# Experts on TensorE: seven f32 products of quarter blocks against three single-pass products of 12-bit parts

## The chip, the cores and the metric

The kernel runs on one core of one Trainium2 chip. The metric is the device time of one execution in microseconds (us), from runs of the unchanged program; lower is better. A separate profiled execution gives the trace. The engines are TensorE (PE; its weight load is listed apart as PEld), VectorE (DVE), ScalarE (ACT), GpSimd (POOL) and SyncE (SP), which issues the transfers.

## What is computed

Two layers work on x of shape (8, 256, 32, 32), all in f32.

```python
# layer 0: softmax attention with a depthwise convolution, then a gated FFN with an 8x8 block FFT filter
x = conv_layer(x, ...)
# layer 1, on tokens t = (8, 1024, 256)
t = t + causal_attention(ln(t), WQ, WK, WV)
z = ln(t)                                     # layer norm over the 256 channels
w = softmax(mean(z, axis=0) @ Wr + br)        # per token position, 8 experts
h = relu(bn1(einsum('bfd,edh->bfeh', z, W1) + b1))
h = relu(bn2(einsum('bfeh,ehk->bfek', h, W2) + b2))
y = einsum('bfeh,ehd->bfed', h, Wo) + bo
t = t + einsum('bfed,fe->bfd', y, w)
```

All 8 experts are computed for all 8192 tokens; each has three 256x256 matrices. The experts' output scaling by w can be done on the second layer's output, because the third layer is linear.

## The kernel before

A tile holds 128 partitions; 256 channels are two groups k of 128 (KC = 2). Work is issued through wrappers (`InOrder`, lines 59 to 73) that keep each of PE, DVE, ACT and POOL in the order in which the code asks for it; most records therefore carry line 71. Transfers are asked for with `nc.sync.dma_start`, all on SyncE's queue, and are not held in this way: a planner places them where their buffers and data are ready.

Layer 0 (lines 476 to 1214) makes the first x. It uses the type F32R for a few products: the scores take queries and keys cut into a high and a low part (`queries_keys`, `stack`, `attend`).

Layer 1's attention (lines 1251 to 1521) goes over 8 images b. `causal(b)` makes scores, exponentials, their normalisation, transposes and the product with the values, row block by row block. Beside it `beside(b)` runs `first_norm(b + 1)`, `second_norm(b - 1)` and `keys_values(b + 1)`. `together(main, side, 0.85)` mixes the two by planned costs that the steps yield: the side gets 0.85 us of its steps per us of the main ones, and what is left of it follows when the main ones are done. `second_norm` makes z = ln(t), stores it to `z_d` and t to `u_d` in device memory, and adds z to `feat` for the gate. The last image is done in halves (`second_norm_half`), then `gate` makes the weights w in `wT`. `load_experts()` loads all 24 expert matrices at the start of this stage.

The experts (lines 1536 to 1769) go over 128 pieces: halves (h, b) of 512 tokens, h outermost, and in each the 8 experts. A piece has `layer1`, `layer2` two pieces later and `layer3` four pieces later; in each pass of the loop at line 1741 four steps of these three are interleaved, and vector work put off in `soon` follows each step. `by_seven` forms a 256x256 by 256x512 product from seven products of 128x128 by 128x256 instead of eight, with sums of the weight blocks (`weight_sums`) and of the column blocks (`column_sums`). Layers 1 and 3 do so for every expert, layer 2 for the odd ones; for even experts layer 2 is four f32 products of 512 columns. Layer 3 adds all 8 experts up in four PSUM banks; `close` then combines them, adds them to t and stores the output. `fetch` loads z and t of a half, three buffers each.

Of the kernel before, what the change touches and what calls it, by code (L numbers as in the profile page):

```python
# [9 lines left out]
F32 = mybir.dt.float32  # L10
F32R = mybir.dt.float32r
BF16 = mybir.dt.bfloat16
# [13 lines left out]
NE = 8  # L26
# [10 lines left out]
MOE_EPS = 1e-3  # L37

# [65 lines left out]
def conv_attn_hybrid_kernel(  # L104
# [1121 lines left out]
    z_d = [dram.tile([P, KC, N], F32, tag=f"zd{b}", name=f"zd{b}") for b in range(B)]  # L1226
# [10 lines left out]
    w_of = []  # L1237
    for e in range(NE):
        w_of.append([])
        for name in ("w1", "w2", "wo"):  # L1240
            w_ = wm.tile([P, KC, C], F32, tag=f"{name}_{e}", name=f"{name}_{e}")
            w_of[e].append(w_)

    def load_experts():
        for e in range(NE):
            for w_, src in zip(w_of[e], (w1, w2, wo)):
                nc.sync.dma_start(w_, src[e].rearrange("(k p) o -> p k o", p=P))
# [3 lines left out]
    with ExitStack() as l1:  # L1251
# [34 lines left out]
        load_experts()  # L1286
# [78 lines left out]
        def second_norm(b):  # L1365
            yield from until((b, N // QC - 1))
            z2 = two.tile([P, KC, N], F32, tag="z2", name="z2", bufs=1)
            yield from layer_norm(b, z2)
            nc.sync.dma_start(z_d[b], z2)
            nc.sync.dma_start(u_d[b], t[b])  # L1370
            if b + 3 < B:
                load_t(b + 3)
            if b == 0:
                pool.tensor_copy(feat, z2)
            else:
                pool.tensor_add(feat, feat, z2)

        def second_norm_half(b, h):
# [6 lines left out]
            nc.sync.dma_start(z_d[b][:, :, hs], z2)  # L1385
            nc.sync.dma_start(u_d[b][:, :, hs], t[b][:, :, hs])
            yield 0.5

# [105 lines left out]
        def beside(b):  # L1494
            if b + 1 < B:
                yield from first_norm(b + 1)
            if b >= 1:
                yield from second_norm(b - 1)
            if b + 1 < B:
                yield from keys_values(b + 1)  # L1500
            else:
                yield from second_norm_half(b, 0)
                yield from gate(0)

# [14 lines left out]
        for steps in (second_norm_half(B - 1, 1), gate(1)):  # L1519
            for _ in steps:  # L1520
                pass
# [14 lines left out]
    with ExitStack() as l2:  # L1536
# [4 lines left out]
        s1, o1 = bn_fold("g1", "be1", "m1", "v1", eps_moe, "bn1", extra="b1")  # L1541
        s2, o2 = bn_fold("g2", "be2", "m2", "v2", eps_moe, "bn2", extra="b2")
# [20 lines left out]
        sums_of = [[None] * 3 for _ in range(NE)]  # L1563

        def seven(e):

            return e % 2 == 1

        def weight_sums(eng, e):

            for l in (0, 1, 2) if seven(e) else (0, 2):
                w_ = w_of[e][l]
                s_ = sums_of[e][l] = hp.tile([P, 3, P], F32, tag=f"ws{e}_{l}", name=f"ws{e}_{l}", bufs=1)
                a11, a21, a12, a22 = (w_[:, k, g * P : (g + 1) * P] for k in range(KC) for g in range(KC))
                eng.tensor_add(s_[:, 0, :], a21, a22)
                eng.tensor_sub(s_[:, 1, :], s_[:, 0, :], a11)
                eng.tensor_sub(a21, a11, a21)
                eng.tensor_sub(s_[:, 2, :], a12, s_[:, 1, :])

        def column_sums(src, name):  # L1580

            T = hp.tile([P, 4, QC], F32, tag=name, name=name, bufs=3 if name == "t2" else 2)
            B4 = src.rearrange("p k (c n) -> p (k c) n", n=QC)
            dve.tensor_sub(T[:, 0:2, :], B4[:, 1::2, :], B4[:, 0:2, :])
            dve.tensor_add(T[:, 2, :], T[:, 1, :], B4[:, 0, :])
            dve.tensor_sub(T[:, 3, :], B4[:, 2, :], T[:, 2, :])
            return T

        def pairs(e, l, src, T):

            w_, s_ = w_of[e][l], sums_of[e][l]
            a11, s3, a12, a22 = (w_[:, k, g * P : (g + 1) * P] for k in range(KC) for g in range(KC))
            b11, b21, b22 = src[:, 0, :QC], src[:, 1, :QC], src[:, 1, QC:]
            return [
                [(s_[:, 0, :], T[:, 0, :]), (a11, b11)],
                [(a12, b21), (s_[:, 1, :], T[:, 2, :])],
                [(s_[:, 2, :], b22), (s3, T[:, 1, :])],
                [(a22, T[:, 3, :])],
            ]

        halves = [(h, b) for h in range(2) for b in range(B)]
        pieces = [(h, b, e) for h, b in halves for e in range(NE)]
        zs, ts, tz, gate_of, bias_of, h1_of, h2_of, acc_of = {}, {}, {}, {}, {}, {}, {}, {}
# [4 lines left out]
        def fetch(i):  # L1608
            if i < len(halves):
                h, b = halves[i]  # L1610
                for of, src, name in ((zs, z_d, "z"), (ts, u_d, "t")):
                    of[h, b] = hp.tile([P, KC, HALF], F32, tag=name, name=f"{name}e", bufs=3)
                    nc.sync.dma_start(of[h, b], src[b][:, :, cut(h)])

        def gate_rows(h, e):

            wb = gate_of[h, e] = hp.tile([P, HALF], F32, tag=f"wb{e}", name=f"wb{e}", bufs=1)
            pw = ps_b.tile([P, HALF], F32, tag="pm", name="pw")
            pe.matmul(pw, sel8[:, e, :], wT[:, cut(h)], start=True, stop=True)
            act.copy(wb, pw)  # L1620

        def gated_bias(h):

            gb = bias_of[h] = hp.tile([P, KC, HALF], F32, tag="gb", name="gb", bufs=1)
            for g in range(KC):
                pw = ps_b.tile([P, HALF], F32, tag="pm", name="pg")
                pe.matmul(pw, boT[:, g, :], wT[:, cut(h)], start=True, stop=True)
                act.copy(gb[:, g, :], pw)

        soon = [[], [], []]  # L1630

        def by_seven(plan, dst, scale, bias, space, tag):

            first = hp.tile([P, 2, QC], F32, tag="first", name="first", bufs=3)

            def of(i):
                pm = space.tile([P, 2, QC], F32, tag=tag, name=f"{tag}{i}")
                for j, (lhs, rhs) in enumerate(plan[i]):
                    pe.matmul(pm[:, j, :], lhs, rhs, start=True, stop=True)
                return pm  # L1640

            def both(x):
                return x.unsqueeze(1).to_broadcast([P, 2, QC])

            act.copy(first, of(0))
            yield
            dve.tensor_add(dst[:, 0:2, :], of(1), both(first[:, 1, :]))
            yield
            dve.tensor_add(dst[:, 2:4, :], of(2), both(dst[:, 1, :]))
            dve.tensor_add(dst[:, 1, :], dst[:, 2, :], first[:, 0, :])  # L1650
            act.activation(dst[:, 0:2, :], dst[:, 0:2, :], AF.Relu, bias=bias[:, 0:1], scale=scale[:, 0:1])
            yield
            dve.tensor_add(dst[:, 2, :], dst[:, 3, :], of(3)[:, 0, :])
            dve.tensor_add(dst[:, 3, :], dst[:, 3, :], first[:, 0, :])
            act.activation(dst[:, 2:4, :], dst[:, 2:4, :], AF.Relu, bias=bias[:, 1:2], scale=scale[:, 1:2])

        def layer1(h, b, e):

            h1 = hp.tile([P, 4, QC], F32, tag="h1", name="h1", bufs=3)
            c = slice(KC * e, KC * e + 2)  # L1660
            yield from by_seven(pairs(e, 0, zs[h, b], tz[h, b]), h1, s1[:, c], o1[:, c], ps_a, "pa")
            h1 = h1.rearrange("p (k c) n -> p k (c n)", k=KC)
            h1_of[h, b, e] = h1, None

            def sums():
                h1_of[h, b, e] = h1, column_sums(h1, "t1")

            if seven(e):
                soon[2].append(sums)
            yield  # L1670

        def layer2(h, b, e):
            h1, T = h1_of.pop((h, b, e))
            h2 = hp.tile([P, KC, HALF], F32, tag="h2", name="h2", bufs=3)
            if seven(e):
                c = slice(KC * e, KC * e + 2)
                h2_4 = h2.rearrange("p k (c n) -> p (k c) n", n=QC)
                yield from by_seven(pairs(e, 1, h1, T), h2_4, s2[:, c], o2[:, c], ps_b, "pm")
            else:
                w_ = w_of[e][1]  # L1680
                for g in range(KC):
                    pm = ps_b.tile([P, HALF], F32, tag="pm", name="pm")
                    for k in range(KC):
                        pe.matmul(pm, w_[:, k, g * P : (g + 1) * P], h1[:, k, :], start=(k == 0), stop=(k == KC - 1))
                    c = KC * e + g
                    act.activation(h2[:, g, :], pm, AF.Relu, bias=o2[:, c : c + 1], scale=s2[:, c : c + 1])
                    if g == 0:
# [194 lines left out]
```

## Time and profile before

| | us |
|---|---|
| median of 3 runs | 3311.7 (3303.55 to 3316.38) |
| profiled execution | 3302.11 |
| its span, first to last instruction | 3300.4 |
| busy in the span: PE / PEld / DVE / ACT / POOL | 3043.3 / 2066.2 / 2346.7 / 1395.4 / 361.1 |
| mean granted TensorE clock | 0.966 |

The busy time of PE counts records whose ends are modelled; it tells where PE has work, not that it is at its peak. In the page's slices each digit is the busy share in tenths of one fortieth of the span (82.5 us): layer 0 fills the first 17, layer 1's attention starts at about 1430 us, and the experts' first product is at 2076.4 us. In a list of groups a line reads: code line, engine, operation, output<-inputs, shapes, count | busy us, mean ns of one | idle us before them and what ended it.

### The profile page before, as it was taken

To read this page: it belongs to the slowest core of one execution; us is meant where nothing else is said; L and a number is where in the kernel's file an instruction comes from. 1 tells how busy PE (TensorE), PEld (TensorE's weight loads), DVE (VectorE), ACT (ScalarE), POOL (GpSimd) and SP (SyncE) were. 2 spreads that over 40 slices of the span, in tenths; PEclk is the share of its full clock that TensorE was granted. 3 is DMA by queue.
4 is the path that set the end of the run, shared out by engine and by line. 5 is a ranking of instruction groups with operands and counts; after the bars stand their busy time and mean duration, and the time that the engine had idled before them with its cause. 6 is when DMAs were issued, how large, how long until landed. Compare 5 with 4: busy or idle time off the path is not lost.

```text
span 3300.4 us, 43194 instructions
## 1 busy us (share of the span) xinstructions
PE 3043.3 (92%) x17462; PEld 2066.2 (63%) x17462; DVE 2346.7 (71%) x3710; ACT 1395.4 (42%) x2168; POOL 361.1 (11%) x482
## 2 busy tenths in 40 slices
PE   5998999999998998769999998999999999999999
PEld 3554555454555455346565665678777777778787
DVE  1377877787877786835544444688888877888887
ACT  2554454545454544323333332344444444444443
POOL 1121212020212010001122212400000000000000
PEclk8998999999999999879999999899999999999999
DMA  4202030303030300030111101100000000000000
GB/s 146 71 8 77 26 77 27 77 27 77 27 77 27 77 14 7 16 136 26 47 44 39 39 26 52 42 24 20 20 20 20 32 16 23 20 20 26 13 7 13
DMA packets 44596, 130.60 MB, mean 40 GB/s; under 512 B 3862, under 2 KB 12134, under 8 KB 40550
## 3 DMA queue, kind: packets, MB, share of 16 engines
q1 hardware_dynamic: 44390, 127.78, 12.5%
q8 instruction: 139, 2.28, 0.3%
q14 instruction: 67, 0.55, 0.1%
HBM read 77.17 MB, written 50.59 MB: 39 GB/s over the span
## 4 chain that ended last, share of the span: by engine, by line
PE 49%; DVE 5%; ACT 1%; POOL 1%; issue 1%; DMA 0%; SPq 0%; ACTq 0%; POOLq 0%; DVEq 0%
PE pm L71 12%; PE pa L71 12%; PE q L71 11%; PE s L71 4%; PE po L71 3%; PE pk L71 2%; PE pv L71 2%; DVE nm L71 1%; DVE zt L71 1%; DVE pr L71 1%; DVE st L71 1%; ACT pr L71 1%; PE tp L71 1%; PE tpz L71 1%; PE tpt L71 1%
## 5 line engine op out<-in xcount | busy, mean ns | idle before, releaser
L71 ACT ACTIVATE h<-h,bn_o,bn_s 128x512 f32<-128x512 f32 x384 | 308.6, 813 | 631.2 <-DVE h L71 631.1
L71 DVE SCALAR_TENSOR_TENSOR x<-hpad,vec,x 128x1024 f32<-128x1024 f32 x248 | 317.1, 1283 | 39.9 <-ACT x L71 32.9
L71 DVE SCALAR_TENSOR_TENSOR conv<-hpad,vec,conv 128x1024 f32<-128x1024 f32 x256 | 329.3, 1293 | 15.4 <-ACT conv L71 8.9
L71 PE MATMUL pm<-h,w 128*128 128x512 f32 (+1 forms) x768 | 318.2, 523 | 0.0
L71 ACT ACTIVATE pT<-s 128x1024 f32<-128x1024 f32 x256 | 247.4, 1024 | 71.8 <-PE s L71 71.8
L71 PE MATMUL po<-pT,vT 128*32 128x256 f32 x4096 | 273.6, 385 | 0.0
L71 PE MATMUL ph<-xn,piw 128*128 128x512 f32 x512 | 244.7, 615 | 3.1 <-DVE xn L71 1.6
L71 PE MATMUL s<-kk,z 128*128 128x512 f32 x512 | 243.0, 602 | 0.6 <-DVE pr L71 0.6
L71 DVE SCALAR_TENSOR_TENSOR o<-vpad,pe_w,o 128x1024 f32<-128x1024 f32 x128 | 163.6, 1283 | 45.6 <-ACT o L71 42.4
L71 PEld LDWEIGHTS pm<-h,w 128*128 128x128 f32 x768 | 146.4, 191 | 75.4 <-issue 61.8
L71 PE MATMUL s<-qst,kst 128*128 128x256 f32 x1024 | 176.0, 314 | 14.6 <-DMA kst<-part 13.2
L71 DVE TENSOR_TENSOR h<-h,wb 128x1024 f32<-128x1024 f32 x128 | 156.8, 1225 | 43.2 <-ACT h L71 43.2
L71 DVE TENSOR_TENSOR h<-pa,first 128x512 f32<-128x512 f32 x128 | 88.3, 690 | 132.6 <-PE pa L71 129.1
L71 PEld LDWEIGHTS po<-pT,vT 128*32 128x32 f32 x4096 | 120.8, 110 | 85.8 <-issue 4.1
L71 DVE TENSOR_TENSOR h<-h,first 128x256 f32<-128x256 f32 x384 | 164.5, 428 | 13.2
L71 PEld LDWEIGHTS s<-qst,kst 128*128 128x128 f32 x1024 | 137.5, 193 | 47.9 <-issue 43.2
L71 ACT ACTIVATE hpad<-ph,pi_o 128x512 f32<-128x512 f32 x126 | 86.8, 689 | 184.6 <-PE ph L71 184.3
L71 PEld LDWEIGHTS ph<-xn,piw 128*128 128x128 f32 x512 | 92.7, 194 | 109.6 <-issue 94.4
L71 PE MATMUL pz<-pow__116,hid 128*128 128x256 f32 x512 | 134.7, 418 | 26.7 <-DVE hid L71 26.7
L71 PE MATMUL sums<-pT,ones 128*32 128x256 f32 x2048 | 158.2, 381 | 0.0
L71 PE MATMUL pa<-tz,ws 128*128 128x256 f32 x512 | 154.6, 384 | 0.0
L71 PE MATMUL pa<-ze,w 128*128 128x256 f32 x512 | 153.3, 382 | 0.0
(264 smaller groups left out, 5792.7 us busy)
## 6 DMA issues: line engine op xcount, KB each, us to landing
qst<-part SPq DMA_DIRECT2D x32, 512.0 KB, 8.7
kst<-part SPq DMA_DIRECT2D x32, 512.0 KB, 15.2
t<-in_x_dram SPq DMA_DIRECT2D x8, 1024.0 KB, 4.8
part<-hi SPq DMA_DIRECT2D x16, 512.0 KB, 2.7
part<-lo SPq DMA_DIRECT2D x16, 512.0 KB, 3.0
td<-t SPq DMA_DIRECT2D x8, 1024.0 KB, 4.9
t<-td SPq DMA_DIRECT2D x8, 1024.0 KB, 4.8
ze<-zd SPq DMA_DIRECT2D x16, 512.0 KB, 3.9
```

The source lines that it names most:

```text
L71: return self._tc.keep_in_program_order(method(*args, **kwargs))
```

## The change

Layers 1 and 3 of the experts are each written as three products on parts with few enough bits for F32R. For a matrix a, part 0 is a scaled by DOWN = 1 - 0.5/4096 and rounded to F32R, part 1 is the rest a - part 0, and part 2 is part 0 - 4096 x part 1. For a weight, part 1 is stored times 4096. A product is then (1 + 1/4096) of the sum of two products (parts 0 with 0, parts 1 with 1) less 1/4096 of the product of parts 2. The first sum and the second product go to banks of their own and are combined when they are evicted. Layer 2 is plain f32 for all experts.

- The parts are three times the data, so the experts are done in two groups of four: visits (G, h, b) of 4 pieces; the first group's output goes to `u_d` and is read again for the second group. Each visit has its own z, now 1.5 MB.
- In layer 1 `second_norm` and `second_norm_half` call `z_parts` for each half, which makes the three parts (one on ACT, two on DVE) and stores them. `expert_parts` makes the parts of W1 and Wo, a matrix at a time, in chores that `beside` takes a few of.
- The first group's weights for expert 0 and one of expert 1, and the first z, are loaded in layer 1; the rest of the group at the start of the experts; the second group's when each tile has been used for the last time.

```diff
-        load_experts()
+        parts_w = two.tile([P, 3, KC, C], F32R, name="parts_w", bufs=1)
+        def expert_parts():
+            for e in range(NE):
+                for l, src in ((0, w1), (1, wo)):
+                    w_ = two.tile([P, KC, C], F32, tag="we", name="we")
+                    nc.sync.dma_start(w_, src[e].rearrange("(k p) o -> p k o", p=P))
+                    yield
+                    upper(parts_w, w_, dve)
+                    lower_part(parts_w, w_)
+                    difference(parts_w)
+                    dve.tensor_scalar_mul(parts_w[:, 1], parts_w[:, 1].bitcast(F32), STEP)
+                    yield
+                    nc.sync.dma_start(w_d[e][l], parts_w.bitcast(F32))
...
@@ second_norm
-            nc.sync.dma_start(z_d[b], z2)
...
+            for h in range(2):
+                yield from z_parts(b, h, z2[:, :, h * HALF : (h + 1) * HALF])
+
+        def z_parts(b, h, src):
+            parts = two.tile([P, 3, KC, HALF], F32R, tag="parts", name="parts", bufs=1)
+            upper(parts, src)
+            yield 1.2
+            lower_part(parts, src)
+            yield 1.2
+            difference(parts)
+            yield 2.4
+            nc.sync.dma_start(z_d[b][:, h], parts.bitcast(F32))
...
@@ beside
             if b + 1 < B:
                 yield from first_norm(b + 1)
+            yield from chore(3)
             if b >= 1:
                 yield from second_norm(b - 1)
+            yield from chore(2)
             if b + 1 < B:
                 yield from keys_values(b + 1)
...
+            yield from chore(2)
...
@@ the experts
+        visits = [(G, h, b) for G in range(NG) for h in range(2) for b in range(B)]
+        pieces = [(v, s) for v in range(len(visits)) for s in range(SLOTS)]
...
+        def products(w_, src, g, both):
+            plan = [(w_[:, 2], src[:, 2])] if both else [(w_[:, 0], src[:, 0]), (w_[:, 1], src[:, 1])]
+            return [(lhs[:, k, g * P : (g + 1) * P], rhs[:, k, :]) for lhs, rhs in plan for k in range(KC)]
...
+        def layer1(v, s):
...
+            for g in range(KC):
+                c = slice(KC * e + g, KC * e + g + 1)
+                for both in (False, True):
+                    pm = ps_a.tile([P, HALF], F32, tag=f"pa{both:d}", name="pa", bufs=1)
+                    plan = products(w_, zs[v], g, both)
+                    for i, (lhs, rhs) in enumerate(plan):
+                        pe.matmul(pm, lhs, rhs, start=(i == 0), stop=(i == len(plan) - 1))
+                    if both:
+                        dve.scalar_tensor_tensor(h1[:, g, :], pm, s1b[:, c], h1[:, g, :], ALU.mult, ALU.add)
+                        soon[2 * g].append(positive(h1[:, g, :]))
+                    else:
+                        act.activation(h1[:, g, :], pm, AF.Identity, bias=o1[:, c], scale=s1a[:, c])
+                    yield
...
@@ layer2, after its products
+            soon[0].append(gated)
+            soon[1].append(lambda: upper(parts, h2))
+            soon[2].append(lambda: lower_part(parts, h2))
+            soon[3].append(lambda: difference(parts))
...
@@ the loop over pieces
+                if s == 1:
+                    fetch_t(v + 1)
+                    if v >= 1:
+                        fetch_z(v + 1)
```

## The prediction, made before the result

> **What bounds the kernel now.** I read the page's slices first, then engine sums by stage, then the groups, the timeline and the SyncE queue of the stage that the change rewrites.
>
> ```profile
> PE   5998999999998998769999998999999999999999
> DVE  1377877787877786835544444688888877888887
> ACT  2554454545454544323333332344444444444443
> 1436.00:2070.00 634.00, 580.70 (x2394) 379.36 (x2394) 305.31 (x814) 195.58 (x355) 121.81 (x174) 0.97 0.13 49
> 2110.00:3286.00 1176.00, 1175.34 (x4897) 927.54 (x4896) 971.76 (x1775) 513.16 (x756) 1.69 (x3) 1.00 0.06 19
> ```
>
> The last two lines are stages (columns: stretch, length, then busy time of PE, its weight load, DVE, ACT, POOL; granted clock, DMA share, GB/s): layer 1's attention, and the experts once they run. In the experts TensorE is idle for 0.7 us of 1176 at full clock: there time is TensorE work, and DVE (83%) and ACT (44%) follow. In layer 1 it is idle for 53 us of 634.
>
> ```profile
> 2600.36 0.59 PE L71 MATMUL q<-t,wo 128*128 128x256 f32 x2
> 2600.79 0.59 PE L71 MATMUL pa<-tz,ws 128*128 128x256 f32 x2
> 2601.22 0.59 PE L71 MATMUL pa<-ze,w 128*128 128x256 f32 x2
> 2088.47 1.88 PE L71 MATMUL pm<-h,w 128*128 128x512 f32 x4
> L71 PE MATMUL q<-h,wo 128*128 128x256 f32 x512 | 151.8, 379 | 0.0
> L71 PEld LDWEIGHTS s<-qst,kst x1024: 186/189/338, 77.2 to 1264.8; 128*128 128x128 f32 x171
> L71 PE MATMUL s<-qst,kst x1024: 274/282/685, 77.3 to 1264.9; 128*128 128x256 f32 x171
> ```
>
> An f32 product of 256 columns is two records, 0.43 us later the next: 0.216 us a record. The f32 512-column products (four records in 1.88 us, the last 0.59) go at 0.43 us a record. The last two lines are layer 0's scores, whose operands are F32R (min/median/max ns): one record per product, 282 ns long where the f32 record over the same 256 columns is 379. So [...] a product of 512 columns in F32R should cost what an f32 record of 256 columns costs, 0.216 us.
>
> [...] The trace has 48 records between 2599.93 and 2610.29 us, 0.2158 each, with a 0.19 us weight load hidden under every one. [...] This trace has one such wait, layer 0's F32R tile with one buffer that must be stored before it is rewritten:
>
> ```profile
> L71 ACT ACTIVATE hi<-pq,qkv_o 128x512 fp32r<-128x512 f32 x32 | 22.0, 689 | 31.3 <-PE pq L71 28.6 <-DMA part<-hi 2.8
> zd<-z SPq DMA_DIRECT2D x7, 1024.0 KB, 3.8
> ud<-t SPq DMA_DIRECT2D x2, 512.0 KB, 3.3
> ```
>
> The change puts the same shape of wait into layer 1, with larger stores.
>
> **The experts, part by part.** A piece is one expert on 512 tokens. Before, an odd expert is 21 products of 256 columns (42 records x 0.2158 = 9.06 us), an even one 14 of these and 4 f32 products of 512 (28 x 0.2158 + 8 x 0.429 = 9.47); mean 9.27. Eight make 74.1 us; the trace's output stores lie 74.2 apart. After, layers 1 and 3 are 12 F32R products of 512 each (24 x 0.2158 = 5.18) and layer 2 is plain f32 (8 x 0.429 = 3.43): 8.61 us. Saved: 0.66 x 128 pieces = **84 us**. The 16 gate-row and 4 bias products stay.
>
> Does another engine become the bound? DVE per piece: two combining operations from PSUM (0.75 each, by layer 0's t<-pp), the gating (1.22), the lower part (1.22), the difference (1.28): 5.2 us, less than before's 7.6 (972/128). ACT: four scaled evictions (0.77), two Relus in place (0.62, by the squares of 512), the upper part over 1024 (1.05 to 1.24): 5.5 us, up from 4.0. Both stay under 8.61. Tightest is h1: its second Relu is queued behind layer 2's eviction, which ends about 8.3 us into the piece, so it ends at 8.9; the next layer 2 begins at 9.5. Cover 0.6 us. Where a visit closes, ACT has two evictions more and DVE two combinations and an addition (about 2.7 us), which could use up the cover: 0 to 0.5 us on each of 32 visits; I take 3 us in all.
>
> Transfers: each visit of 34.4 us moves 1.5 MB of z parts, 0.5 in and 0.5 out, 73 GB/s; the burst at 2072 us moved 351 GB/s. z has two buffers and is fetched when a buffer falls free, a visit ahead: 34 us of cover for about 5. Weights of group two (7.3 MB) replace each slot after its last use; three pieces (26 us) cover 3 to 5 us each. At the start 4.7 MB of weights, two t and a z come after layer 1's memory is free: 7.2 MB, 21 us at 350 GB/s, while the first z and four weight tiles lie ready and the pieces use the rest in the order it arrives. Before, DVE and POOL made weight sums there and PE lost 3 us up to 2110. I take 0, bounds -4 to +10. The end: the chain behind the last product was 7 us, four additions shorter after; but the last piece's parts take 5.6 us of DVE and ACT while PE has 2.6 us of layer 3: +1 together.
>
> **Layer 1, which pays.** Added: per half image one ACT operation (1.1), two on DVE (1.22 + 1.28) and a store of 1.5 MB in place of 0.5, 16 times; per expert and layer a load, four DVE operations over 512 columns (0.69 for the two-operand ones; the scalings 0.35 to 0.95 by the 256-column scaling of 0.42 to 0.49, I take 0.7: 2.8 in all) and a 0.75 MB store, 16 times. DVE gains 40 + 45 us on 305 of 634, ACT 18 on 196: sums with room. The price is order. The parts tile has one buffer, so ACT's upper part of the second half waits for the first half's store. It is queued 4.8 planned us later, over 0.85 thus 5.6; the parts are ready about 4.5 us after the first upper part, the store takes about 5 (estimate from 3.3 at 0.5 MB and 3.8 at 1 MB), so ACT stands for some 4 us in each of 7 batches. Behind it: the exponentials and the evictions of the transposes; PE has a score block (3.45 us) that needs neither. I take 1 us a batch, 7; bounds 0 and 28. DVE bursts of 2.8 us stand before row maxima and the normalisation scaling, which PE already awaits (tpz<-zt, 25.7 us in seven batches): 0.3 us each, 5; bounds 0 and 20. The initial burst of 24 weight loads goes; nothing on PE waited for it. The last parts before the second gate lie beside its 6 us of logit products: 0, up to 5 where they are late. Layer 1: **+12 us**, bounds -5 and +50.
>
> **Sum.** -84 + 3 + 1 + 12 = -68 us. From the profiled execution's 3302.1 (span 3300.4) that gives 3234. The median of the runs is 3311.7, 9.6 above the profiled one; the same step from it gives **3243**, which I forecast, since it is the median that is compared. All gains at their bound give about 3215; all costs at theirs at once 3309, all but one or two of them 3290. So 3215 to 3290.
>
> **Rivals.**
> 1. Layer 1 gives most of it back: all ACT and DVE waits exposed, +50 to +85 us, net -33 to 0: 3279 to 3312. For it: in-order queues, a single parts buffer. Against: PE awaits DVE for only 38 of 634 us now, and the row chain has about 6 us of slack in long rows. 0.10.
> 2. Slower, by SyncE's queue. The code asks for t of the next visit before z, and t must wait until the visit before last has closed and stored. If z stands behind t in the queue, it lands about 14 us after PE needs it (close 4 us into the visit, two transfers of 2.7, z 5): 31 x 14 = +430 us, near 3670. It decides from 2.7 us a visit (84/31). Against it:
>
> ```profile
> 2142.91 0.52 SPq L1613 DMA_DIRECT2D ze<-zd  x1
> 2188.51 0.40 SPq L1733 DMA_DIRECT2D out_dram<-te  x1
> 2191.27 0.52 SPq L1613 DMA_DIRECT2D te<-ud  x1
> ```
>
> There the output store goes ahead of the te load that the code asks for earlier, and ze goes when its buffer falls free: the queue's order is by readiness. 0.07.
> 3. The change doesn't do what it says: products of F32R tiles of 512 columns run as two double passes. 24 x 0.858 + 3.4 = 24 us a piece, +1900 us. The 282 ns row speaks against it. 0.02.
> 4. Layer 1 pays nothing and the start gains: -90, 3222; inside the range. 0.06.
>
> The forecast has 0.75. A change under 0.5% (17 us), about what a measurement of this kernel can tell from none, comes from the end of rival 1: 0.04. Faster by more: 0.75 + 0.06 + 0.06 = 0.87. Slower: 0.07 + 0.02 = 0.09. About 0.1 lies above 3290 and a little below 3215.
>
> **What would show it.** Right: F32R records of pa and q of 379 ns, 12 per piece and layer; output stores 34.4 us apart in the second group; PE over 99% busy in the experts; layer 1's batches (74.4 us apart now) 1 to 3 us longer, with ACT waiting on the parts' store. Wrong: TensorE idle before pa behind the z load; ACT or DVE over 90% busy in the experts; batches longer than 80 us.

## The result, and the profile after

The changed kernel takes **3327.3 us** (median of 8 runs, 3321.5 to 3338.3) beside 3309.5 for the kernel before (8 runs, 3300.5 to 3316.4): a ratio of 1.0056 with a 95% interval of 1.0038 to 1.0073. It is slower, by half a per cent; the forecast was 3243. The profiled executions have spans of 3326.3 and 3300.4 us, so the traces account for 25.9 us where the medians differ by 17.8: the profiled execution of before is one of its shorter ones, and the terms below add up to the 25.9.

TensorE's slices and three stages of the kernel after, as they were shown of before (slices of 83.2 us here; PEclk is the granted TensorE clock; a stage's columns are stretch, length, busy PE, weight load, DVE, ACT, POOL, then clock, DMA share, GB/s):

```profile
PE   5998899998989898679898888699999999999999
PEclk8998999999999999889999999799999999999999
1436.00:2070.00 634.00, 561.51 (x2190) 353.71 (x2189) 357.50 (x844) 196.95 (x346) 116.03 (x157) 0.94 0.23 87
2070.00:2142.00 72.00, 45.92 (x205) 36.65 (x205) 34.02 (x68) 15.36 (x26) 13.75 (x18) 0.74 0.27 107
2310.00:3300.00 990.00, 990.00 (x3500) 655.99 (x3499) 613.39 (x634) 592.02 (x829) 0.00 (x0) 1.00 0.23 78
```

The experts (last line) are what was forecast in kind: TensorE is never idle, DVE and ACT are at 62% and 60%. Layer 1 (first stage line) is not: PE was idle for 53 of these 634 us before and is idle for 72 now, at a clock of 0.94 instead of 0.97, and the stage has not ended at 2070 but at 2142.

Four marks cut every trace into the parts that matter: the first product pa<-lin in layer 0 at 1322 us, behind which the change begins; the last product po of layer 1's attention; the first product pa of the experts; and the end. The first mark itself falls at 1316.3 to 1324.9 us in the executions of this document, so a difference of a few us between two spans says nothing of the change. All in us:

| kernel | layer 1 | gap to experts | experts | span |
|---|---|---|---|---|
| before | 727.8 | 26.8 | 1224.0 | 3300.4 |
| after | 787.9 | 34.3 | 1182.5 | 3326.3 |

So layer 1 lost 60, the gap 7.5, and the experts gained 41.5, which makes the 25.9 us within 0.2. Forecast were about +12 for layer 1, 0 for the gap and -80 for the experts with their closings and end. Both large terms were off, and both to the slower side.

**Layer 1.** The waits between 1430 and 2142 us (who waited for what: us in total, times, longest), and the group of ScalarE's first operation of z's parts:

```profile
ACT parts L72 <- DMA zd<-parts: 45.0, 7, 8.7
DVE parts L72 <- ACT parts L72: 31.3, 7, 5.9
PE pk L72 <- ACT kk L72: 32.7, 6, 7.8
PE po L72 <- ACT pT L72: 10.1, 2, 9.9
L72 ACT ACTIVATE parts<-z 128x1024 fp32r<-128x1024 f32 x16 | 16.9, 1058 | 45.1 <-DMA zd<-parts 45.0
```

The store wait of the prediction is there, seven times, 6.4 us on average where some 4 were estimated. TensorE, for which the prediction had 1 us a batch, stands about as long: 32.7 us before pk in six batches, up to 9.9 before po in the last. One batch in the timeline, the one with the longest wait (start, length, engine, operation, idle before it and its releaser):

```profile
1741.15 1.06 ACT L72 ACTIVATE parts<-z 128x1024 fp32r<-128x1024 f32 x1
1741.33 4.54 POOL L72 TENSOR_TENSOR feat<-feat,z 128x2048 f32<-128x2048 f32 x1 [1.35 <-ACT z L72]
1743.53 3.42 DVE L72 TENSOR_TENSOR parts<-z,parts 128x1024 fp32r<-128x1024 f32 x1
1745.76 3.60 PE L72 MATMUL s<-kk,z 128*128 128x512 f32 x8
1748.32 15.13 SPq L1430 DMA_DIRECT2D zd<-parts  x2
1749.86 3.60 PE L72 MATMUL pk<-z,at 128*128 128x512 f32 x8
1755.31 1.06 ACT L72 ACTIVATE parts<-z 128x1024 fp32r<-128x1024 f32 x1 [8.70 <-DMA zd<-parts]
1756.40 1.23 DVE L72 TENSOR_TENSOR parts<-z,parts 128x1024 fp32r<-128x1024 f32 x1 [5.87 <-ACT parts L72]
1757.54 1.22 DVE L72 TENSOR_REDUCE nm<-s 128x1 f32<-128x1024 f32 x1
1758.85 1.11 ACT L72 ACTIVATE pr<-s,nm 128x1024 f32<-128x1024 f32 x1 [2.48 <-DVE nm L72]
1760.59 1.10 ACT L72 COPY kk<-pk 128x512 f32<-128x512 f32 x2
1761.25 6.03 PE L72 MATMUL pk<-z,at 128*128 128x512 f32 x8 [7.80 <-ACT kk L72]
```

Read it from the top. The first half's upper part is made at 1741.15, but its lower part starts only at 1743.53 and takes 3.42 us beside GpSimd's addition (1.23 for the second half at 1756.40): the parts are ready at 1748.2, 7 us after the first upper part and not 4.5. The store takes 6.9 us until 1755.2; in five of the seven batches it took 5.1 to 5.2. ScalarE stands from 1746.61 on. TensorE still has a score block and the eight records of pk, which end at 1753.46, and then needs kk's eviction. That stands in ScalarE's queue behind the second upper part, behind an exponential which waits for DVE's row maximum, which itself was queued on DVE behind the second lower part. So the eviction comes 5.3 us after the wait is over (1755.31 to 1760.59), and TensorE's wait follows from the walk: 8.7 us of ScalarE's wait, 5.3 of the queue and 0.6 of the eviction, less 6.85 of cover, are the 7.8 that it stood. Then the same eight records of pk take 6.03 instead of 3.60 us, since the clock is down (0.64 granted between 1761 and 1768, 0.50 in the first 3.25 us of these records; they begin 0.85 us apart at first and 0.43 at the end). The stores ud<-t lie 83.3 us apart on average from 1551.67 to 2051.39; before, 73.8.

**The gap.** The first half's gate used to lie beside the last attention products; now it follows them. Before, then after (logit products lg, attention products po):

```profile
2040.22 0.61 PE L71 MATMUL lg<-wrs,feat 128*128 128x8 f32 x4
2041.57 8.34 PE L71 MATMUL po<-pT,v 128*128 128x256 f32 x32
```

```profile
2103.08 6.75 PE L72 MATMUL po<-pT,v 128*128 128x256 f32 x32 [0.24 <-ACT pT L72]
2112.77 0.61 PE L72 MATMUL lg<-wrs,feat 128*128 128x8 f32 x4 [2.06 <-DVE feat L72]
```

The side work of the last image grew by the planned steps of parts and chores ahead of that gate, and what is left of it runs when the main work is done. That these steps are the reason is argued and not shown: no run here brings that gate back ahead of the last attention products.

**The experts.** The final output stores:

```profile
2831.72 0.39 SPq L1742 DMA_DIRECT2D out_dram<-te  x1
2867.61 0.39 SPq L1742 DMA_DIRECT2D out_dram<-te  x1
```

They lie 35.89 us apart, not 34.4: 8.97 us a piece, not 8.61. The eight f32 records of layer 2 go at 0.4285 us a step, as forecast. The 24 F32R products thus take 5.54 us, 0.231 each, where the prediction had put 0.2158. A sign of it lay in the trace of before: layer 0's scores are F32R products of 256 columns, and one group of eight reads

```profile
85.26 1.21 PE L71 MATMUL s<-qst,kst 128*128 128x256 f32 x8
```

In that group the starts lie 117 to 120 ns apart behind the first one, which is more than half of 0.2158; the prediction read only how long such a record lasts.

### The profile page after: what moved, and what is told of

The parts are those of the page before. It is cut to its first block, busy times and chain, and to the rows that moved or that the text cites. A ratio compares the mean times of both kernels' runs of the same rounds, so it can differ in the third digit from the quotient of the medians.

```text
span 3326.3 us, 40817 instructions
## 1 busy us (share of the span) xinstructions
PE 3027.1 (91%) x16566; PEld 1899.6 (57%) x16566; DVE 2155.4 (65%) x2728; ACT 1577.8 (47%) x2376; POOL 328.8 (10%) x410
## 4 chain that ended last, share of the span: by engine, by line
PE 45%; DVE 6%; ACT 2%; DMA 1%; issue 1%; POOL 1%; SPq 0%; ACTq 0%; POOLq 0%; DVEq 0%
PE pm L72 13%; PE pa L72 11%; PE q L72 10%; PE s L72 3%; PE po L72 3%; PE pv L72 2%; PE pk L72 1%; DVE nm L72 1%; DMA zd<-parts 1%; DVE parts L72 1%; ACT pr L72 1%; DVE zt L72 1%; DVE pr L72 1%; DVE st L72 1%; PE tpt L72 1%
## 5 line engine op out<-in xcount | busy, mean ns | idle before, releaser
L72 PE MATMUL q<-h2p,w 128*128 128x512 f32 x1536 | 538.3, 460 | 0.5 <-DVE h2p L72 0.5
L72 PE MATMUL pm<-h,w 128*128 128x512 f32 x1024 | 480.9, 591 | 1.0 <-ACT h L72 1.0
L72 PE MATMUL pa<-ze,w 128*128 128x512 f32 x1488 | 423.9, 393 | 0.0
L72 DVE SCALAR_TENSOR_TENSOR h<-pa,s1b,h 128x512 f32<-128x512 f32 x256 | 191.8, 749 | 326.3 <-PE pa L72 318.3
L72 PEld LDWEIGHTS q<-h2p,w 128*128 128x128 f32 x1536 | 289.3, 188 | 167.0 <-issue 119.6
L72 PEld LDWEIGHTS pa<-ze,w 128*128 128x128 f32 x1488 | 278.3, 188 | 72.3 <-issue 9.1
L72 ACT ACTIVATE h<-pm,bn_o,bn_s 128x512 f32<-128x512 f32 x256 | 199.5, 779 | 194.4 <-PE pm L72 118.1
L72 ACT ACTIVATE h<-pa,bn_o,s1a 128x512 f32<-128x512 f32 x256 | 198.3, 775 | 196.1 <-PE pa L72 196.0
L72 PEld LDWEIGHTS pm<-h,w 128*128 128x128 f32 x1024 | 192.6, 188 | 145.8 <-issue 122.6
L72 DVE TENSOR_TENSOR h2p<-h,h2p 128x1024 fp32r<-128x1024 f32 x128 | 156.5, 1222 | 22.7 <-ACT h2p L72 18.2
```

The source lines that it names most:

```text
L72: return self._tc.keep_in_program_order(method(*args, **kwargs))
```

## The experiments

The experiments ask two questions: is it the store wait that costs layer 1 its 60 us, or the added operations; and why does an F32R product cost 0.231 us? Each run of a whole kernel was timed beside the kernel before (medians 3306.8 to 3311.0 in the four sets). "Layer 1", "gap" and "experts" are cut by the marks above, from one profiled execution each.

| run | median us | ratio to before, 95% | layer 1 | gap | experts |
|---|---|---|---|---|---|
| two_parts | 3278.5 | 0.9899 to 0.9932 | 737.8 | 34.9 | 1181.8 |
| apart | 3289.4 | 0.9930 to 0.9967 | 747.7 | 34.9 | 1181.9 |
| z_plain | 3267.2 | 0.9858 to 0.9891 | 726.5 | 34.3 | 1182.5 |
| no_wparts | 3323.0 | 1.0030 to 1.0063 | 782.2 | 35.2 | 1183.1 |
| bare | 3268.7 | 0.9853 to 0.9888 | 727.6 | 35.2 | 1183.1 |
| combined | 3281.9 | 0.9913 to 0.9940 | 729.2 | 43.7 | 1183.1 |
| placed | 3274.4 | 0.9885 to 0.9914 | 733.6 | 34.5 | 1182.3 |
| f32_run | 3281.5 | 0.9906 to 0.9934 | 737.8 | 34.9 | 1186.0 |
| best | 3274.6 | 0.9890 to 0.9917 | 732.8 | 34.1 | 1185.9 |
| best2 | 3459.1 | 1.0433 to 1.0465 | 730.7 | 34.9 | 1366.9 |

**1. two_parts: a second buffer.**

```diff
-            parts = two.tile([P, 3, KC, HALF], F32R, tag="parts", name="parts", bufs=1)
+            parts = two.tile([P, 3, KC, HALF], F32R, tag="parts", name="parts", bufs=2)
```

> The parts tile of layer 1 gets a second buffer; nothing else changes. Theory A (the single buffer costs the 60 to 70 us that layer 1 grew by: ACT stands at the second half's upper part until the first half is stored, 45 us in 7 waits, TensorE is idle for 43 us behind it and then starts at half clock): the waits of ACT on the store go from 45 us to under 5, TensorE's idle pk<-kk and po<-pT waits from 43 us to under 5, and the time falls by 45 to 65 us, from 3327 to about 3270, below the kernel before. Rival B (the added vector work and the pushed-back keys and values make the layer longer, and the wait only shows where the time would be lost anyway): the time falls by less than 15 us, the batches stay over 81 us.

Measured: 3278.5 us, 49 less than after (46 by the two ratios) and 0.8% faster than before. The wait is gone from the group, with its operations unchanged, and the clock of layer 1 is back (two_parts, group between 1430 and 2142, and a stage; then layer 1 between its marks, in after and in two_parts):

```profile
L72 ACT ACTIVATE parts<-z 128x1024 fp32r<-128x1024 f32 x16 | 17.0, 1064 | 0.1
1436.00:2030.00 594.00, 546.91 (x2210) 349.39 (x2209) 362.01 (x848) 198.80 (x350) 126.41 (x159) 0.98 0.23 91
1321.70:2109.60 787.90, 662.09 (x2518) 415.91 (x2519) 459.31 (x968) 235.85 (x410) 126.23 (x170) 0.92 0.21 80
1319.40:2057.20 737.80, 642.87 (x2518) 408.14 (x2519) 459.53 (x968) 235.50 (x410) 132.00 (x170) 0.95 0.22 85
```

Layer 1 falls by 50 of the 60 us it had lost. The last two lines say how: with the same records on every engine, TensorE is idle for 31 us less (125.8 to 94.9) and its own records take 19 us less (662.1 to 642.9). So the waits cost their length and, in the slower restart, more than half as much again. One sign of theory A was missed: TensorE's waits before pk and po did not fall under 5 us but to 12.2. With the wait for this one store the kernel is slower than before; without it, it is faster.

**2. apart: the same buffer, another place.** The second half's parts are made after keys_values.

```diff
-            for h in range(2):
-                yield from z_parts(b, h, z2[:, :, h * HALF : (h + 1) * HALF])
+            yield from z_parts(b, 0, z2[:, :, :HALF])
...
                 yield from keys_values(b + 1)
+            if b >= 1:
+                yield from z_parts(b - 1, 1, held[b - 1][:, :, HALF:])
```

> The kernel after with one parts buffer as it is, but the second half's parts are made after keys_values instead of right behind the first half's. Theory A (the wait for the store was a matter of place, not of memory: 33 us of keys and values between the halves cover the 10 us from the first half's last part to the end of its store): six of the seven 8.7 us stands of ACT are gone, in the last batch two remain (second half of image 6, then image 7); so some 6/7 of the 49 us that the second buffer saved: 3280 to 3292. Rival (the second buffer helped in another way, for instance by letting DVE run ahead): no better than the kernel after, 3315 to 3330.

Measured: 3289.4 us, in the range of theory A. One wait is left in the waits of ScalarE in this run, and its layer 1 is 40 us shorter than after's:

```profile
ACT parts L72 <- DMA zd<-parts: 6.8, 1, 6.8
```

So it was the order in the queue that cost, and memory is only one way to repair it, though here the better one by 10 us of layer 1.

**3. z_plain, no_wparts, bare: the operations alone.** z_plain stores z three times in place of its parts, no_wparts does so with the weights, bare with both.

```diff
-            upper(parts, src)
...
-            nc.sync.dma_start(z_d[b][:, h], parts.bitcast(F32))
+            for r in range(3):
+                nc.sync.dma_start(z_d[b][:, h, r], src)
+            yield 4.8
...
-                    upper(parts_w, w_, dve)
...
-                    nc.sync.dma_start(w_d[e][l], parts_w.bitcast(F32))
+                    for r in range(3):
+                        nc.sync.dma_start(w_d[e][l][:, r], w_)
```

> Leaves out the making of z's parts: z itself is stored three times in place of its parts (the same 1.5 MB, the same planned 4.8 us, no parts tile), so the output is not the reference's. Theory A: as two_parts, within 10 us of it, since two DVE operations and one ACT operation per half are cheap once nobody waits for the store. Rival B: clearly faster than two_parts, by 25 us or more, the price of the operations themselves.

> Leaves out the making of the weights' parts: each loaded matrix is stored three times in place of its parts, no DVE operation, so the output is not the reference's. The single parts buffer for z stays. Theory A: the chores hardly matter: DVE waits 20 us for their stores but TensorE shows no idle time for it; 0 to 8 us less than 3327. Rival B (DVE is held by the chores, which delays row maxima and normalisation): 20 us less or more.

> The kernel after without any making of parts in layer 1: z and the weights are stored three times in place of their three parts (so the experts compute something else, with the same instructions); the stores and loads stay. What it is faster than before by is then what the experts' new form is worth by itself, with its start and the longer tail. By the trace of after the experts gained 41.6 us: 3262 to 3268. By my prediction's price of an F32R product it would be 80: 3225 to 3235. Against z stored plain with the weights' parts still made (3267): if the weights' chores cost what they did in no_wparts (4 us), 3261 to 3265; if DVE's work there is hidden, 3266 to 3268.

Measured: 3267.2, 3323.0 and 3268.7 us. Against two_parts, z_plain shows what z's parts cost once the wait is gone: 11 us, a little over the 10 of theory A. no_wparts puts the weights' chores at 4 us by the medians and at 6 by layer 1, beside the wait, which is not clear of noise (the intervals of its ratio and of after's overlap); bare against z_plain puts them at nothing (3268.7 to 3267.2, the ranges overlap). In bare, layer 1 is as long as before (727.6 to 727.8) with all the added stores and loads in it, so that traffic costs nothing there. bare has the experts' new form and no other cost than the gap: it is 42 us faster than before by the medians (3311.0 in its set), 32 by the traces, and not the 80 of the forecast.

**4. micro: products alone.** Twelve stretches of products without the kernel, some with DVE, ACT, GpSimd or transfers busy beside them.

```diff
+    for i in range(n):
+        pe.matmul(bank[:, :cols], lhs[:, j, :], rhs[:, (i // 8) % 2, c : c + cols], start=True, stop=True)
```

> Not the layers: twelve stretches of products alone, with other work beside some of them; the output is a copy. It asks why an F32R product of 512 columns took 231 ns a piece in the experts and not 216. Theory C (fixed price of the operands): 96 F32R products of 512 columns with nothing beside them already take 228 to 234 ns from one to the next, and the stretches with DVE, ACT and transfers beside are the same within 2 ns. Rival D (other engines' traffic in SBUF): 216 to 218 ns alone, 225 or more with DVE and ACT beside. Rival E (the weight load): 216 where all products of a stretch have the same stationary operand at one address, and F32R of 256 columns stays over 130 ns. f32 products of 256 columns: 216 ns a record in every case.

Three stretches of its timeline: F32R over 512 columns, six settings one after the other (one stationary operand throughout, then DVE, ACT, transfers, and mixtures of these beside); f32 over 256 columns with DVE, ACT and transfers beside; F32R beside GpSimd:

```profile
84.86 131.17 PE L72 MATMUL acc<-r,wr 128*128 128x512 f32 x576
215.86 20.88 PE L72 MATMUL acc<-t,w 128*128 128x256 f32 x96
236.39 22.12 PE L72 MATMUL acc<-r,wr 128*128 128x512 f32 x96
```

From start to start: (215.86 - 84.86) / 576 = 0.2274 us for an F32R product, (236.39 - 215.86) / 96 = 0.214 for an f32 record (0.2158 inside the stretch). In all six settings the usual step is 227 ns, just under the range of theory C. Over 256 columns an F32R product steps at 113 to 120 ns, not at the 130 and more of rival E. So the step does not change with the stationary operand (each product has its weight load in either case) or with other work beside it, and neither D nor E is borne out; it is 5% above that of the f32 record over half the columns. Of the 0.015 us that the forecast lacked, 0.0115 are this; 0.004 were still open. (This run and the next are one execution each.)

**5. micro2: f32 and F32R in turn.** Groups of products in the kernel's proportions, no other work beside them.

```diff
+    piece(6, [("f", 512, 4, 2), ("r", 512, 24, 4)], True)
...
+    piece(12, [("f", 512, 2, 2), ("r", 512, 12, 4)], True)
```

> Not the layers: seven stretches of TensorE products alone. 96 F32R products of 512 columns; the same accumulated in fours; six times 4 f32 products of 512 and 24 F32R, accumulated; the same without accumulation; twelve times 2 f32 of 512 and 12 F32R, accumulated; twelve times 4 f32 of 256 and 12 F32R; six times 4 f32 of 512 and 24 F32R of 256 columns. It asks where 227 ns (alone) becomes 231 in the experts. Theory A (the switch from f32 products to F32R ones costs, over the next ten or so): stretches 1 and 2 at 227, 3 to 6 at 230 to 235 in the mean, more with the shorter runs. Theory B (accumulating in a bank costs): stretches 2, 3, 5 and 6 at 231, 4 at 227. Theory C (neither; it is the reading of PSUM beside it): all at 227.

Two cycles of its timeline: four f32 products (8 records) and 24 F32R; two f32 products (4 records) and 12 F32R:

```profile
62.48 3.59 PE L72 MATMUL acc<-t,w 128*128 128x512 f32 x8
65.51 6.02 PE L72 MATMUL acc<-r,wr 128*128 128x512 f32 x24
71.36 3.59 PE L72 MATMUL acc<-t,w 128*128 128x512 f32 x8
...
164.72 1.88 PE L72 MATMUL acc<-t,w 128*128 128x512 f32 x4
166.03 3.33 PE L72 MATMUL acc<-r,wr 128*128 128x512 f32 x12
169.20 1.88 PE L72 MATMUL acc<-t,w 128*128 128x512 f32 x4
```

The first cycle is 71.36 - 62.48 = 8.88 us; two of the second are 2 x (169.20 - 164.72) = 8.96, the kernel's 8.97 within 0.01. Accumulation alone left the step at 227 ns. Behind 8 f32 records only the first F32R steps are longer (232 and 231 ns, then 226 to 229), also where the records are 256 columns; behind 4, nine of eleven are at 228 to 236. So theory A holds, with a narrower condition than it named: not every switch costs, only one after a short run of f32 records. Why four records are too few, no run here tells, and it is not the only cause of such steps: in f32_run below, steps of 224 to 236 ns also stand behind a stall of 0.2 us.

**6. combined and placed: what is left in layer 1.** Both start from two_parts and take the chores in pairs; combined moves GpSimd's addition behind the parts and each gate ahead of its half's parts, placed moves only the addition, behind the chores.

```diff
-            yield from chore(3)
+            yield from chore(2)
...
+            elif b > 1:
+                pool.tensor_add(feat, feat, held[b - 1])
...
@@ combined alone, in second_norm_half
+            yield from gate(h)
             yield from z_parts(b, h, z2)
```

> The kernel with two parts buffers, and three placements: the chores in pairs instead of three at a time, so that two matrices' parts are never made back to back (DVE stood 20.9 us in six waits for the store of parts_w); GpSimd's addition of z to feat behind the parts instead of beside the first lower part (which took 3.42 us there and 1.23 elsewhere, in 7 batches); each half's gate ahead of that half's parts in the last image. If DVE's order in layer 1 is what still separates it from the kernel with z stored plain (11 us), most of that comes back: 3264 to 3274. If DVE's bursts are covered and only the tail counts, 3272 to 3278. If the added products of the gate hold back the main ones, or GpSimd's addition only clashes with something else: 3278 or more.

> The kernel with two parts buffers, with two of the three placements of the run named combined: the chores in pairs, and GpSimd's addition of z to feat, now behind the chores that follow the parts. The gates stay behind the parts. Theory A (in combined the pairs won some 7 us in layer 1, last t store 2051.0 instead of 2058.2, and the gate ahead of the last parts lost 9 at the start of the experts, because the experts' tiles lie in memory that the last parts' store still reads: sel waited 21.4 us for it): 3268 to 3274, first product pa 33 to 35 us behind the last t store. Rival (the pairs gained nothing, and the tail only moved): 3277 to 3282.

Measured: 3281.9 and 3274.4 us. In combined layer 1 came back by 8.6 of the 11 us, but the gap grew by 9, so nothing was won: the third case of what was expected, by a cause it did not name. In combined's groups:

```profile
L72 DVE SCALAR_TENSOR_TENSOR parts_w<-parts_w 128x512 fp32r<-128x512 f32 x16 | 25.3, 1578 | 0.5
L1612 POOL MEMSET sel<- 8x1024 f32 x1 | 0.9, 942 | 21.4 <-DMA zd<-parts 21.4
```

The second line is the reason: the experts' first tiles take over memory that the last parts' store still reads. The last gate's products are issued at 2080.1 us, but the parts are made behind it and their store has landed only at 2089.5; sel is set after that, and TensorE stood 10.2 us for it. With the gates back behind the parts (placed) the gap to the experts is 34.5 again. The first line shows that the clash with GpSimd's addition only moved: the weights' difference takes 1.58 us in the mean there, 0.69 in two_parts. In combined the first half's gate stands ahead of its parts and still follows the last attention products, so it leaves open what moved that gate. placed is 4 us faster than two_parts by the medians and in layer 1, where 7 were expected; that is just over theory A's range, and the intervals of the two ratios overlap, so the gain is likely but not clear of noise. placed is, with best, the fastest kernel here that leaves nothing out: 1.0% under before.

**7. f32_run, best, best2: longer runs of f32.** f32_run is two_parts with layer 2's four products in one step; best is placed with the same; best2 also makes h2's upper part one step later.

```diff
+            yield
             for g in range(KC):
...
                 act.activation(h2[:, g, :], pm, AF.Relu, bias=o2[:, c : c + 1], scale=s2[:, c : c + 1])
-                yield
-                if g == 0:
-                    yield
+            yield
+            yield
...
@@ best2 alone
-            soon[1].append(lambda: upper(parts, h2))
-            soon[2].append(lambda: lower_part(parts, h2))
+            soon[2].append(lambda: upper(parts, h2))
+            soon[3].append(lambda: lower_part(parts, h2))
```

> The kernel with two parts buffers, with layer 2's four f32 products of a piece (eight records) issued in one step instead of two and two in different steps. In the run of products alone, 8 f32 records and 24 F32R products took 3.03 + 5.86 = 8.89 us, 2 x (4 f32 records and 12 F32R) 2 x (1.31 + 3.17) = 8.97 us, which is the experts' 8.97. Theory A (short runs of f32 records are what makes the F32R products behind them 231 ns instead of 227): pieces of 8.89 us, output stores 35.5 apart instead of 35.89, 128 x 0.085 = 11 us off: 3265 to 3272. Rival (the 4 ns come from work beside TensorE, and the agreement is chance): 3276 to 3281, stores still 35.9 apart. Third case (layer 2 in one step makes the next evictions late): slower than 3281, with TensorE waits in the experts.

> Both of the two runs before in one kernel. If both gains hold they add up, 11 + 7 off 3278: 3256 to 3265. If only one holds, 3266 to 3273.

> The kernel of the run named best, with ScalarE's upper part of h2 one step later (behind layer 1's eviction of that step, not ahead of it). In f32_run and best three pieces of a visit took 8.887 us, as in the run of products alone, but the closing one 9.233: its first product of pa waited 0.2 us and its second 0.1 for a bank that ScalarE had not yet emptied, because two layer 2 evictions, a copy of a closing sum and an upper part were queued ahead. That gave back all that the longer f32 runs won. Theory A (that queue is the cause): stores 35.55 us apart instead of 35.89, 32 x 0.34 = 11 us off best's 3274.6: 3262 to 3267. Rival (the closing piece is long for another reason): 3272 to 3278, stores still 35.9 apart. Third case: the later lower part comes too late for layer 3, with TensorE waiting for h2p: above 3278.

Measured: 3281.5, 3274.6 and 3459.1 us. In f32_run the pieces that close no visit take 8.887 us, as in micro2, so the 4 ns come from the short runs of f32. But the kernel is no faster, as in the third case of what was expected: the piece that closes a visit takes 9.23, and 3 x 8.887 + 9.233 = 35.89, as in two_parts to the hundredth. The end is longer too: the last output store comes 22.7 us behind the one before it, 18.9 in two_parts. There, in f32_run between 2310 and 3230 us (25 closings in it):

```profile
PEld pa L72 <- ACT h L72: 12.4, 25, 0.8
2708.39 0.76 PEld L72 LDWEIGHTS pa<-ze,w 128*128 128x128 f32 x4 [0.46 <-ACT h L72]
```

pa's bank is not yet emptied: in the timeline ScalarE has a layer 2 eviction, a closing sum's copy and h2's upper part directly ahead of it (2705.21 to 2707.67). That this queue is the reason was to be shown by best2, and was not. The third case of its expectation came: the later parts of h2 came too late for layer 3, and pieces took 10.0 us and more (waits of TensorE between 2310 and 3400 us):

```profile
PE q L72 <- DVE h2p L72: 80.2, 94, 1.8
```

These waits are under half of the 181 us that best2's experts lose to best's; the rest was not taken apart. So that run says only that the parts of h2 have no slack of a whole step. best (3274.6) is level with placed and above both of its ranges: the longer f32 runs added nothing. Whether the closing could be mended otherwise was not tried.

## Why the prediction was wrong, point by point

- **Sign.** 3243 was forecast, 3327 measured; the range ended at 3290. Two terms were mis-sized together: layer 1 and the gap cost 67.6 us instead of 12, the experts gave 41.5 instead of 80. The two main errors, the store wait (43 us) and the price of an F32R product (47), are about equal. By estimate, taking either out of the measured 3327 leaves 3280 to 3284, under before's 3309, so the sign needed both.
- **"I take 1 us a batch, 7; bounds 0 and 28"** (the store wait) is the first step that failed: it cost 50 us by two_parts, 7 a batch. The wait itself was foreseen, on the right engine and at the right place; in the batch shown ScalarE reached it 5.46 us after the first upper part, as worked out (5.6). One input was off: the parts were ready after 7 us in six batches, 5.8 in the first, instead of 4.5, because DVE came to them late and, in those six, its operation took 1.81 to 3.42 us beside GpSimd's addition and not 1.22. The store's 5 us were right in five batches of seven (6.9 in two). The larger error is in turning ScalarE's wait into TensorE's. "PE has a score block that needs neither" was true and too modest, since pk followed it: 6.85 us of cover in the batch shown. But after the wait the queue still has to run up to the eviction that TensorE needs, through DVE and back (5.3 us), and then TensorE restarts at a lower clock (0.50 granted for 3.25 us). The upper bound of 28 was ScalarE's own wait times seven; what is queued behind a wait can cost more than the wait.
- **DVE bursts, 5 us**: z's parts cost 11 and the chores between 0 and 6, within the bounds. Right in kind, low.
- **The start, 0 us**: +7.5, and bare shows it (35.2) without any parts made, so the added operations are not its cause. In the traces the gate of the first half slid behind the last product; what moved it stays open. The weights and z were there in time, as said. "The last parts before the second gate: 0" looked at the wrong gate.
- **"a product of 512 columns in F32R should cost what an f32 record of 256 columns costs, 0.216 us"** is the second step that failed: 0.227 alone, 0.231 in the kernel's order. 24 x 128 x 0.0152 = 47 us, more than half of the gain. The prediction used the length of an F32R record (282 ns), not a step between two of them, which its own trace had (117 to 120 ns for 256 columns); the equality was the author's estimate, which no trace showed, and should have carried bounds of its own. With it the pieces save 84 - 47 = 37 us; the stores give (9.275 - 8.973) x 128 = 39.
- **Closings +3, end +1**: the rest of the experts is 2.8 us shorter (41.5 - 38.7), not 4 longer. Pieces of after take the same 8.97 us whether a visit closes or not.
- **Rival 1** (layer 1 gives most of it back, +50 to +85) is what happened in layer 1; its total of 3279 to 3312 took the 84 of the experts as given and so fell short. Its reason against, that PE awaited DVE for only 38 us before, said nothing of a wait on ScalarE that the change itself adds. **Rival 2** (z behind t in SyncE's queue) is refuted: no wait for z or t in the experts. **Rival 3** is refuted by 227 ns. **Rival 4** (no cost in layer 1, a gain at the start) came true in neither half: even bare keeps the gap.
- **"Wrong: batches longer than 80 us"** was the sign that showed: 83.3. Of the signs of being right, TensorE over 99% busy in the experts came, and the stores 34.4 us apart did not.
- **The range.** The bounds as given add up to about 3305 and 3220, not 3309 and 3215; both slips are small beside 3327.

## What to carry to other kernels

A wait put at the head of an in-order queue is priced by walking that queue to the next instruction that the bounding engine needs, through every other queue it passes, and adding the slower restart (here 19 us beside 31 of idle time); the length of the wait alone is not an upper bound. A single buffer between a producer and a long store needs either a second buffer or as much other work between its uses as the store takes; here the one gave back 50 of the 60 us of layer 1, the other 40. When a saving is many times a small price, measure that price from start to start, back to back and in the kernel's own order, before building on it: 11 and 4 ns decided over 47 us.

## What the runs showed of the hardware

- An F32R product over 512 columns steps at 227 ns alone (micro, six settings), an f32 record over 256 columns at 216 (micro; 0.2158 us in before). How many bits F32R keeps, on which the parts rest, no run here measures: that theirs are few enough was the author's assumption.
- After four f32 records the F32R products behind them step at 224 to 236 ns (after, experts; micro2), after eight at 227 from the third or fourth on (micro2). The uneven steps stand behind a stall of 0.2 us too (f32_run).
- After 7.8 us without work eight records of pk took 6.03 us, otherwise 3.60; the steps between records are 0.85 us there and 0.43 otherwise, half the rate, and the granted clock was 0.50 from 1761.25 to 1764.5 us. The same showed behind all six waits of pk, of which the shortest is 2.95 us (start at 1591.63): eight records took 5.35 to 6.73 us, with 0.50 to 0.55 granted in the first 2.6 us and more. So each of these waits cost more than its length.
- DVE's operation parts<-z,parts took 3.42 us beside GpSimd's addition and 1.23 without (after, at 1743.53 and 1756.40). The addition began at 1741.33 and ended at 1745.87, the DVE operation at 1746.95. In all six batches with the addition beside it, the DVE operation took 1.81 to 3.42 us and ended 1.08 us after the addition, which itself took 4.51 to 4.54. In combined, where the addition stands behind the parts, the same DVE operation takes 1.22 us in the mean of 16, against 1.89 in two_parts, and the weights' difference 1.58 against 0.69.
